# Turning the gated layer's state by block transposes and a trip through DRAM instead of TensorE

## The chip, the cores and the metric

The kernel runs on one core of a Trainium2 chip. A core has TensorE (PE; its weight loads are shown apart as PEld), VectorE (DVE), ScalarE (ACT), GpSimd (POOL) and SyncE (SP, which here only issues transfers). They run at the same time, each takes its own instructions in order, and they wait for each other by semaphores. The metric is the device time of one execution in microseconds.

## The reference

There are 64 graphs of 256 nodes with 128 features, and one dense adjacency matrix of 256 x 256 with numbers in fp32. Four layers follow each other, and each is added to its normed input's source:

```python
h = maximum(layernorm(x), 0)                       # before every layer
# layer 0: five steps of a gated layer
m  = adj @ h                                       # the same for both inputs of the concatenation
z  = sigmoid([m, m] @ w3.T + b3 + h @ u3.T + bu3)
r  = sigmoid([m, m] @ w4.T + b4 + h @ u3.T + bu3)
hv = tanh([m, m] @ w5.T + b5 + (r * h) @ u5.T + bu5)
h  = (1 - z) * h + z * hv
# layer 1: Chebyshev hops of adj up to order 2, then @ Theta1, relu
# layer 2: (adj @ h + h) @ weight + bias, divided by the row's norm
# layer 3: pairwise attention
pre  = s1[i, :] + s2[j, :] + b_lin                 # 256 x 256 x 256 numbers for each graph
e    = leaky_relu(pre, 0.2) @ a + adj
out  = sigmoid(softmax(e) @ h)
```

Layer 3 forms 256 numbers for every pair of nodes of every graph. It is by far the largest part.

## The kernel before, in words

The 64 graphs go in 32 pairs (`NB = 2`). A tensor is held in one of two layouts. By token (`tok`), the partitions are nodes, and the free dimensions are graph of the pair, half of the nodes and feature. By feature (`feat`), the partitions are the 128 features, and the free dimensions are graph and node: 512 numbers in each partition, one PSUM bank.

**The tiles.** Layer 3 is worked in tiles of 128 x 2048 numbers, 128 for each pair and 4096 in all. A tile takes four nodes i, both graphs, all nodes j and one half k of the 256 hidden numbers. It is made by one of three engines: by VectorE in one instruction (line 652, `min` of two operands, the first half k = 0 only), by ScalarE in eight (line 665, either half; from `s2c` for the first half, from a PSUM copy of `s2n` for the second), or by GpSimd in eight (line 672, second half only). TensorE then multiplies it with a window of the vector a and adds it to the scores (line 709, four groups of 32 columns side by side). There are 13 tile buffers; VectorE may hold 8 of them, ScalarE 3 and GpSimd 2.

**The fronts.** Everything before layer 3 is `front(p)`, a generator that goes through layers 0 to 2 for pair p and then makes layer 3's operands. One step of the gated layer goes like this: `mix_nodes` multiplies the state h, by token, with `adj_t` and gives m by feature (TensorE, line 264); ScalarE copies it to mT (line 341); `project` runs five products of 512 columns (line 264); ScalarE applies three tanh (lines 381, 396, 399); VectorE runs four elementwise operations of 512 numbers a partition: rh (line 385), d (line 404), the product with z (line 408) and the new state hT (line 412). The new state is by feature, and the next `mix_nodes` needs it by token as its stationary operand. `to_token` turns it with four 128 x 128 transposes on TensorE (line 292), and ScalarE copies it from PSUM (line 423). The last of the five steps needs the turn for another reason: its result is added to x by token (line 428).

**The tails.** When all 64 tiles of a block of 128 nodes are scored, `tail` adds adj, takes the softmax (lines 558 to 571), turns the weights (line 292), multiplies and stores the result (line 604). There are two tails for each pair. The store's source `o` has two buffers.

**The order.** A planner inside the kernel writes it by hand when the program is built. It keeps a clock for each engine, with a cost for every step (`PROJECT`, `TURN`, `COPY`, `ELEMENTS` and so on). A front or a tail yields before each step the engine it needs and the time from which it can run. When an engine is free the planner takes a tail's step first, then a front's, then a tile. `chain_ready` holds a front back that is more than two steps ahead of its due place, so that it is spread over 1.7 pairs' time. Up to two fronts are under way beside the tiles. `in_order` then ties each engine's instructions to this order. So the order and the share of tiles of each engine are fixed in the program; only the real durations decide how it runs.

**Transfers.** All x loads (line 146), the load of `adj_n` (line 158) and the stores are issued by SP, in the program's order. `xin` has two buffers; `load_x(p + 1)` is called when front p begins. The weights come by ScalarE's queue at the start.

The functions that the change touches, with the profile's line numbers:

Of the kernel before, what the change touches and what calls it, by code (L numbers as in the profile page):

```python
# [8 lines left out]
F32 = mybir.dt.float32  # L9
# [5 lines left out]
P = 128  # L15
NB = 2
STEPS = 5
# [3 lines left out]
PE, DVE, ACT, POOL = ENGINES = (mybir.EngineType.PE, mybir.EngineType.DVE, mybir.EngineType.Activation, mybir.EngineType.Pool)  # L21
# [4 lines left out]
def kernel(  # L26
# [50 lines left out]
    nc = tc.nc  # L77
    B, N, D = x.shape
    NC = N // P
# [4 lines left out]
    const = ctx.enter_context(tc.tile_pool(name="const", bufs=1))  # L84
    work = ctx.enter_context(tc.tile_pool(name="work", bufs=2))
    relu_pool = ctx.enter_context(tc.tile_pool(name="relu", bufs=3))
    psum = ctx.enter_context(tc.tile_pool(name="psum", bufs=1, space=PSUM))
    banks = [psum.tile([P, NB * N], F32, name=f"bank{k}") for k in range(8)]
    s2v = banks[:2]
    s2p = banks[2].rearrange("p (b n) -> p b n", b=NB)  # L90
# [1 line left out]


    clock = dict.fromkeys((PE, DVE, ACT, POOL), 0.0)
    SEEN = {PE: 0.25, DVE: 0.14, ACT: 0.18, POOL: 0.13}
    behind = [0.0]

    def ran(engine, us, *after):
        start = max(clock[engine], 0.0, *after)
        if engine == ACT:  # L100
            behind[0] = max(0.0, behind[0] - (start - clock[ACT])) + 0.024 * us
        clock[engine] = start + us
        return clock[engine] + SEEN[engine] + (behind[0] if engine == ACT else 0.0)

    spare = [[b, 0.0] for b in banks[5:]]

# [5 lines left out]
    def by_feature(b):  # L112
        return b.rearrange("p (b n) -> p b n", b=NB)

    def by_token(b):
        return b.rearrange("p (b c n) -> p b c n", b=NB, c=NC)

    def bank(shape, name):

        spare.append(spare.pop(0))  # L120
        return spare[-1][0][:, :shape[1]]
# [19 lines left out]
    def load_x(p):  # L141
        if p >= NPAIR:
            return
        XIN[p] = work.tile([P, NB, NC, D], F32, name="xin", bufs=2)
        for b in range(NB):
            nc.sync.dma_start(XIN[p][:, b], x[p * NB + b].rearrange("(c p) d -> p c d", p=P))

    load_x(0)


    ident = const.tile([P, P], F32, name="ident")
# [7 lines left out]
    adj_t = const.tile([P, NC, N], F32, name="adj_t")  # L159
    adj_ti = const.tile([P, NC, N], F32, name="adj_ti")  # L160
    for c in range(NC):
        pt = bank([P, N], "pt")
        for k in range(NC):
            nc.tensor.transpose(pt[:, k * P:(k + 1) * P], adj_n[:, k, c * P:(c + 1) * P], ident)
        nc.vector.tensor_copy(adj_t[:, c, :], pt)
        nc.vector.tensor_copy(adj_ti[:, c, :], adj_t[:, c, :])
        nc.vector.tensor_add(adj_ti[:, c, c * P:(c + 1) * P], adj_t[:, c, c * P:(c + 1) * P], ident)


    adj_2 = const.tile([P, NC, N], F32, name="adj_2")  # L170
    for c in range(NC):
        pt = bank([P, N], "pt")
# [76 lines left out]
    pt = bank([P, P], "pt")  # L249
# [16 lines left out]
    def flat(t):  # L266
        return t.rearrange("p b n -> p (b n)")
# [5 lines left out]
    def mix_nodes(pm, h, a):  # L273

        pm = by_feature(pm)
        for b in range(NB):
            for c in range(NC):
                side_by_side(pm[:, b, :], h[:, b, c, :], a[:, c, :], c == 0, c == NC - 1)

    def to_feature(pt, h):  # L280

        pt = by_token(pt)
        for b in range(NB):
            for c in range(NC):
                nc.tensor.transpose(pt[:, b, c, :], h[:, b, c, :], ident)  # L285
# [25 lines left out]
    SHORT = dict(tag="short", bufs=12)  # L311
# [3 lines left out]
    COPY, BIASED, TANH, ELEMENTS = 0.48, 0.58, 0.57, 0.61  # L315
# [34 lines left out]
    def front(p):  # L350
# [7 lines left out]
        h = tok("h", **SHORT)  # L358
        t = yield from norm(x0, 0.0, h)
        yield PE, t, 1  # L360
        b = take()
        to_feature(b[0], h)
        t_h = t
        t = ran(PE, TURN, t, b[1])
        yield ACT, t
        hT, t_hT = copied("hT", b, t)
        for step in range(STEPS):
            yield PE, t_h, 1
            b = take()
            mix_nodes(b[0], h, adj_t)  # L370
            t = ran(PE, MIX, t_h, b[1])
            yield ACT, t
            mT, t_m = copied("mT", b, t)
            yield PE, t_m, 1
            pr = take()
            project(pr[0], u3t, hT, stop=False)
            project(pr[0], w4t, mT, start=False)
            t = ran(PE, 2 * PROJECT, t_m, t_hT, pr[1])
            yield ACT, t, 1
            r = take()  # L380
            nc.scalar.activation(r[0], pr[0], AF.Tanh, bias=br, scale=0.5)  # L381
            t = ran(ACT, TANH, t, r[1])
            yield DVE, t
            rh = feat("rh", **SHORT)
            nc.vector.scalar_tensor_tensor(rh, by_feature(r[0]), 1.0, hT, op0=OP.add, op1=OP.mult)  # L385
            t_rh = ran(DVE, ELEMENTS, t)
            spare.append([r[0], t_rh])
            yield PE, t_rh, 1
            project(pr[0], w34, mT, start=False)
            t_z = ran(PE, PROJECT, t)  # L390
            pv = take()
            project(pv[0], w5t, mT, stop=False)
            project(pv[0], u5t, rh, start=False)
            t = ran(PE, 2 * PROJECT, t_rh, pv[1])
            yield ACT, t_z
            nc.scalar.activation(pr[0], pr[0], AF.Tanh, bias=bz, scale=0.5)  # L396
            t_z = ran(ACT, TANH, t_z)
            yield ACT, t
            nc.scalar.activation(pv[0], pv[0], AF.Tanh, bias=bh, scale=1.0)  # L399
            t = ran(ACT, TANH, t)  # L400

            yield DVE, t
            d = feat("d", **SHORT)
            nc.vector.tensor_sub(d, by_feature(pv[0]), hT)  # L404
            t = ran(DVE, ELEMENTS, t)
            spare.append([pv[0], t])
            yield DVE, max(t_z, clock[DVE])
            nc.vector.scalar_tensor_tensor(by_feature(pr[0]), by_feature(pr[0]), 1.0, d, op0=OP.add, op1=OP.mult)  # L408
            ran(DVE, ELEMENTS, t_z)
            yield DVE, clock[DVE]  # L410
            hT_new = feat("hT", bufs=4)
            nc.vector.scalar_tensor_tensor(hT_new, by_feature(pr[0]), 0.5, hT, op0=OP.mult, op1=OP.add)  # L412
            hT = hT_new
            t_hT = ran(DVE, ELEMENTS)
            spare.append([pr[0], t_hT])
            yield PE, t_hT, 1
            b = take()
            to_token(b[0], hT)
            t = ran(PE, TURN, t_hT, b[1])
            if step < STEPS - 1:  # L420
                yield ACT, t
                h = tok("h", **SHORT)
                nc.scalar.copy(h, by_token(b[0]))  # L423
                t_h = ran(ACT, COPY, t)
                spare.append([b[0], t_h])
# [2 lines left out]
        nc.vector.tensor_add(x1, x0, by_token(b[0]))  # L428
        t = ran(DVE, ELEMENTS, t)
        spare.append([b[0], t])  # L430


        h = tok("h", **SHORT)
        t_h = yield from norm(x1, t, h)
        yield PE, t_h, 1
        b = take()
        mix_nodes(b[0], h, adj_n)
        t = ran(PE, MIX, t_h, b[1])
# [3 lines left out]
        b = take()  # L442
        to_feature(b[0], h)
        t = ran(PE, TURN, t_h, b[1])
        yield ACT, t
        hT, t = copied("hT", b, t)
        yield PE, t_h, 1
        b = take()
        mix_nodes(b[0], h, adj_2)
        t = ran(PE, MIX, t_h, b[1])  # L450
        yield ACT, t
        c2T, t = copied("c2T", b, t)
# [3 lines left out]
        t = ran(PE, PRODUCTS, t, po[1])  # L456
        yield DVE, t
        pt = rows_of(by_token(po[0]))
# [5 lines left out]
        t = ran(DVE, ELEMENTS)  # L464
# [3 lines left out]
        h = tok("h", **SHORT)  # L468
        t = yield from norm(x2, t, h)
        yield PE, t, 1  # L470
        b = take()
        mix_nodes(b[0], h, adj_ti)
        t = ran(PE, MIX, t, b[1])
        yield ACT, t
        yT, t = copied("yT", b, t)
# [3 lines left out]
        t = ran(PE, PRODUCT, t, po[1])  # L479
        yield DVE, t  # L480
        pt = rows_of(by_token(po[0]))
        nc.vector.tensor_add(pt, pt, bias2.unsqueeze(1).to_broadcast([P, NB * NC, D]))
        t = ran(DVE, ELEMENTS, t)
# [3 lines left out]
        t = ran(ACT, COPY, t)  # L487
# [3 lines left out]
        t = ran(DVE, ELEMENTS, t)  # L491
        yield POOL, t
        inverse_root(rn, OP.max, NORM_EPS * NORM_EPS)
        t = ran(POOL, 1.25, t)
# [3 lines left out]
        for k in range(NB * NC):  # L498
            nc.vector.scalar_tensor_tensor(rows_of(x3)[:, k], pt[:, k], rn[:, k:k + 1], rows_of(x2)[:, k],
                                           op0=OP.mult, op1=OP.add)  # L500
        t = ran(DVE, 1.04, t)
# [4 lines left out]
        t = yield from norm(x3, t, h3)  # L506
        yield PE, t, 1
        b = take()
        to_feature(b[0], h3)
        t = ran(PE, TURN, t, b[1])  # L510
        yield ACT, t
        hT, t_hT = copied("hT3", b, t)
# [9 lines left out]
        b = take()  # L522
        project(b[0], g2, hT)
        t = ran(PE, PROJECT, t_hT, b[1])
# [3 lines left out]
        b = take()  # L528
        project(b[0], w2n[:, P:2 * P], hT)
        t = ran(PE, PROJECT, t_hT, b[1])  # L530
# [3 lines left out]
        b = take()  # L534
        project(b[0], adj_t[:, 0, P:2 * P], hT)
        t = ran(PE, PROJECT, t_hT, b[1])
# [6 lines left out]
        b = take()  # L543
        project(b[0], adj_t[:, 0, 0:P], hT)
        t = ran(PE, PROJECT, t_hT, b[1])
# [6 lines left out]
                        since=(max(t_n, t_s2a, t_s2c), max(t_b, t_2)))  # L552
# [172 lines left out]

    def begin_front():
        p = begun_fronts[0]
        load_x(p + 1)
        begin(p, front(p))
        begun_fronts[0] += 1  # L730

# [18 lines left out]

    in_order()
    now = dict.fromkeys(clock, 0.0)
    for e in clock:
        clock[e] = 0.0
    while scored[0] < 2 * NSLOT or CHAINS:
# [4 lines left out]
        for key in CHAINS:  # L760
            since = chain_ready(key, e)
# [6 lines left out]
        else:  # L768
            since = tile_ready(e)
# [47 lines left out]
```

## Time and profile before

| | |
|---|---|
| median of three timed runs | 5358.55 us (5358.25 to 5358.73) |
| the profiled execution | 5354.23 us, of it the span 5352.4 us |
| TensorE clock granted, mean | 0.996 |
| PE busy | 5241.4 us |
| DVE busy | 5221.7 us |
| POOL busy | 5160.9 us |
| ACT busy | 5121.4 us |
| moved by transfers | 26.99 MB, 5 GB/s |

The span is the time from the first to the last instruction of the profiled execution. Busy is the time in which an engine has at least one instruction running. Instructions of one engine overlap a little: the end of one is recorded after the next has begun. So a mean duration is longer than the distance from one start to the next, and where an engine is full the distance is what counts.

### The profile page before, as it was taken

The numbers are of one execution on the slowest core, as the hardware profiler recorded it, in microseconds if no ns is written. First come the engines' busy times: TensorE is split into PE (matmuls) and PEld (weight loads), VectorE is DVE, ScalarE is ACT, GpSimd is POOL, SyncE is SP. The second block draws the span as 40 slices with busy tenths as digits, with TensorE's granted clock in tenths as the row PEclk, the third lists the DMA queues.
The fourth block names the chain that finished last, engine by engine and source line by source line (L and its number), as shares of the span: only waits on it lengthen the run. The fifth ranks groups of instructions, "written<-read, shape, count | busy, mean of one in ns | idle before, by whom it ended". The sixth has DMA issues, their size and how long they took to land.

```text
span 5352.4 us, 138977 instructions
## 1 busy us (share of the span) xinstructions
PE 5241.4 (98%) x56085; PEld 1861.5 (35%) x56085; DVE 5221.7 (98%) x4322; ACT 5121.4 (96%) x13465; POOL 5160.9 (96%) x5974
## 2 busy tenths in 40 slices
PE   6999999999999999999999999999999999999998
PEld 2333333333333333333333333333333333333332
DVE  3999999999999999999999999999999999999998
ACT  3999999999999999999999999999999999999999
POOL 0999999999999999999999999999999999999999
PEclk9999999999999999999999999999999999999999
DMA  0000000000000000000000000000000000000000
GB/s 17 5 5 6 6 3 6 6 5 6 5 4 6 5 6 5 3 6 6 5 5 4 4 6 5 6 6 3 6 5 6 6 5 3 6 5 4 4 2 4
DMA packets 38839, 26.99 MB, mean 5 GB/s; under 512 B 3504, under 2 KB 38192, under 8 KB 38192
## 3 DMA queue, kind: packets, MB, share of 16 engines
q1 hardware_dynamic: 35088, 17.05, 1.1%
q8 instruction: 438, 7.18, 0.6%
q14 instruction: 209, 1.71, 0.1%
q10 hardware_dynamic: 3104, 1.05, 0.1%
HBM read 9.70 MB, written 8.39 MB: 3 GB/s over the span
## 4 chain that ended last, share of the span: by engine, by line
PE 49%; DVE 34%; POOL 9%; ACT 5%; issue 4%; DMA 0%; POOLq 0%; SPq 0%; DVEq 0%; ACTq 0%
PE bank L709 32%; DVE rl L652 28%; PE bank L264 15%; POOL rl L672 7%; ACT rl L665 3%; PE bank L292 1%; DVE d L404 1%; DVE stats L324 1%; DVE bank L408 1%; DVE hT L412 1%; DVE rh L385 1%; PE bank L285 1%; POOL sc L562 0%; DVE mv L327 0%; POOL mv L259 0%
## 5 line engine op out<-in xcount | busy, mean ns | idle before, releaser
L672 POOL TENSOR_SCALAR rl<-s2n,s1b 128x256 f32<-128x256 f32 x5328 | 4786.0, 940 | 9.7 <-ACT s1b L539 9.7
L652 DVE TENSOR_TENSOR rl<-s1a,bank 128x2048 f32<-128x2048 f32 x2015 | 4484.6, 2276 | 12.1 <-ACT s1a L548 12.1
L665 ACT ACTIVATE rl<-bank,s1b 128x256 f32<-128x256 f32 x11056 | 4392.2, 839 | 1.3
L709 PE MATMUL bank<-rl,win_n 128*32 128x512 f32 x21448 | 2654.8, 593 | 33.9 <-DVE rl L652 31.9
L709 PE MATMUL bank<-rl,win 128*32 128x512 f32 x11320 | 1487.2, 593 | 0.0
L709 PEld LDWEIGHTS bank<-rl,win_n 128*32 128x32 f32 x21448 | 678.9, 110 | 1496.4 <-issue 1214.0
L709 PEld LDWEIGHTS bank<-rl,win 128*32 128x32 f32 x11320 | 365.9, 110 | 754.4 <-issue 630.2
L264 PE MATMUL bank<-adj_t,h 128*32 128x256 f32 x5120 | 310.0, 381 | 3.8 <-ACT h L423 3.8
L264 PEld LDWEIGHTS bank<-adj_t,h 128*32 128x32 f32 x5120 | 166.6, 110 | 174.3 <-issue 58.6
L335 ACT ACTIVATE h<-x,mv 128x128 f32<-128x128 f32 x384 | 172.1, 634 | 43.3 <-POOL mv L331 42.9
L264 PE MATMUL bank<-hT,u3t 128*32 128x512 f32 x1280 | 169.5, 593 | 0.0
L264 PE MATMUL bank<-mT,w4t 128*32 128x512 f32 x1280 | 169.4, 592 | 0.0
L264 PE MATMUL bank<-mT,w 128*32 128x512 f32 x1280 | 166.8, 593 | 0.5 <-ACT bank L381 0.5
L264 PE MATMUL bank<-mT,w5t 128*32 128x512 f32 x1280 | 166.7, 592 | 0.4 <-DVE rh L385 0.4
L264 PE MATMUL bank<-rh,u5t 128*32 128x512 f32 x1280 | 166.6, 592 | 0.0
L341 ACT COPY mT<-bank 128x512 f32<-128x512 f32 x160 | 133.9, 837 | 33.1 <-PE bank L264 24.6
L396 ACT ACTIVATE bank<-bank,gate_b 128x512 f32<-128x512 f32 x160 | 141.0, 881 | 17.7 <-PE bank L264 17.7
L381 ACT ACTIVATE bank<-bank,gate_b 128x512 f32<-128x512 f32 x160 | 140.0, 875 | 15.6 <-PE bank L264 15.2
L399 ACT ACTIVATE bank<-bank,gate_b 128x512 f32<-128x512 f32 x160 | 136.3, 852 | 12.8 <-PE bank L264 12.8
L423 ACT COPY h<-bank 128x512 f32<-128x512 f32 x128 | 117.3, 916 | 29.6 <-PE bank L292 24.7
L258 POOL TENSOR_SCALAR mv<-mv 128x4 f32<-128x4 f32 x128 | 29.8, 232 | 120.1 <-DVE mv L326 112.5
L404 DVE TENSOR_TENSOR d<-bank,hT 128x512 f32<-128x512 f32 x160 | 108.4, 678 | 37.5 <-ACT bank L399 37.5
(116 smaller groups left out, 3445.0 us busy)
## 6 DMA issues: line engine op xcount, KB each, us to landing
xin<-in_x_dram SPq DMA_DIRECT2D x64, 128.0 KB, 2.3
out_dram<-o SPq DMA_DIRECT2D x64, 128.0 KB, 1.8
w_raw<-in_L_gnn_w_w_dram ACTq DMA_DIRECT2D x3, 128.0 KB, 4.3
th_raw<-in_L_gnn_Theta_dram ACTq DMA_DIRECT2D x1, 320.0 KB, 3.1
adj_n<-in_adj_dram SPq DMA_DIRECT2D x1, 256.0 KB, 4.8
w_raw<-in_L_gnn_u_w_dram ACTq DMA_DIRECT2D x2, 64.0 KB, 3.4
bias<-in_L_gnn_bias_dram ACTq DMA_DIRECT2D x2, 64.0 KB, 3.0
w<-in_L_gnn_weight_dram ACTq DMA_DIRECT2D x1, 64.0 KB, 2.8
```

The costliest lines, as they stand in the source:

```text
L264: nc.tensor.matmul(o[g:g + 32], w[:, g:g + 32], t, start=start, stop=stop, skip_group_check=True)
L335: nc.scalar.activation(h[:, k, :], s[:, k, :], AF.Relu, bias=mv[:, k, 0:1], scale=mv[:, k, 1:2])
L341: nc.scalar.copy(c, by_feature(bank[0]))
L381: nc.scalar.activation(r[0], pr[0], AF.Tanh, bias=br, scale=0.5)
L396: nc.scalar.activation(pr[0], pr[0], AF.Tanh, bias=bz, scale=0.5)
L399: nc.scalar.activation(pv[0], pv[0], AF.Tanh, bias=bh, scale=1.0)
L404: nc.vector.tensor_sub(d, by_feature(pv[0]), hT)
L423: nc.scalar.copy(h, by_token(b[0]))
L652: nc.vector.tensor_tensor(t, rows.to_broadcast(whole), ops["s2a"].unsqueeze(1).to_broadcast(whole), op=OP.min)
L665: nc.scalar.activation(t[:, g, b, :], (s2p if k else ops["s2c"])[:, b, :], AF.Relu, bias=ops["s1"][k][:, b, i:i + 1], scale=-1.0)
L672: nc.gpsimd.tensor_scalar(t[:, part, b, :], ops["s2n"][:, b, :], ops["s1"][1][:, b, i:i + 1], None, op0=OP.min)
L709: nc.tensor.matmul(pe[g * 32:(g + 1) * 32, :], w[:, k, 31 - r:63 - r], flat(t[:, g]), start=first, stop=(left[block] == 0), skip_group_che ...
```

## The change

Two pairs, p = 0 and 1, keep the old way. For all others, the first four steps of the gated layer no longer use `to_token` and ScalarE's copy. The new function `turned` takes hT, transposes it in blocks of 32 x 32 on VectorE (`blocks`, line 314 of the changed kernel), writes the result to a DRAM buffer (`moves`, line 317) and reads it back in another order (`h_turned`, line 320), so that each partition holds one node of each group of 128. Both transfers are issued by SP. The nodes end up in another order within a group: partition 4 i + c holds node 32 c + i. So `mix_turned` (line 303) multiplies with `adj_p`, a copy of `adj_t` whose rows are put in that order by a product with the permutation `places` during the set-up. It issues as many matmuls of the same size as `mix_nodes`.

The planner books the transpose with `ELEMENTS` (0.61) on VectorE and each transfer with `moved`, 0.5 us of a queue and 2.2 more until the data are there. `blocks` has one buffer, so the planner keeps a transpose until the write before it has been done.

The x loads move as well: the first two pairs' are issued at the very start, ahead of `adj_n`, and `load_x(p + 2)` stands where front p has used its x for the last time.

```diff
+    dram = ctx.enter_context(tc.tile_pool(name="dram", bufs=4, space=bass.MemoryType.DRAM))
...
+    def moved(since):
+        queue[0] = max(queue[0], since) + 0.5
+        return queue[0] + 2.2
...
     load_x(0)
+    load_x(1)
...
+    adj_p = const.tile([P, NC, N], F32, name="adj_p")
+    places = const.tile([P, P], F32, name="places")
+    nc.vector.tensor_copy(places.rearrange("p (i c) -> p i c", c=4), ident.rearrange("p (c i) -> p i c", c=4))
+    for c in range(NC):
+        pt = bank([P, N], "pt")
+        nc.tensor.matmul(pt, places, adj_t[:, c, :])
+        nc.vector.tensor_copy(adj_p[:, c, :], pt)
...
+    def mix_turned(pm, h, a):
+        pm = by_feature(pm)
+        for b in range(NB):
+            for c in range(NC):
+                for g in range(4):
+                    nc.tensor.matmul(pm[g * 32:(g + 1) * 32, b, :], h[:, g, b * NC + c, :], a[:, c, :],
+                                     start=(c == 0), stop=(c == NC - 1), skip_group_check=True)
+
+    t_turn = [0.0]
+
+    def turned(ht, since):
+        yield DVE, max(since, t_turn[0])
+        blocks = work.tile([P, 4, NB * NC, 32], F32, name="blocks", bufs=1)
+        nc.vector.transpose(blocks, flat(ht).rearrange("p (m c j) -> p c m j", c=4, j=32))
+        t = ran(DVE, ELEMENTS, since)
+        moves = dram.tile([P, 4 * P], F32, name="moves")
+        nc.sync.dma_start(moves, blocks.rearrange("p c m j -> p (c m j)"))
+        t_turn[0] = moved(t)
+        h = work.tile([P, 4, NB * NC, 32], F32, name="h_turned", **SHORT)
+        nc.sync.dma_start(h.rearrange("p a m j -> p a (m j)"), moves.rearrange("(a i) (c x) -> (i c) a x", a=4, c=4))
+        return h, moved(t_turn[0])
...
-            mix_nodes(b[0], h, adj_t)
+            if step > 0 and p >= 2:
+                mix_turned(b[0], h, adj_p)
+            else:
+                mix_nodes(b[0], h, adj_t)
...
+            if step < STEPS - 1 and p >= 2:
+                h, t_h = yield from turned(hT, t_hT)
+                continue
             yield PE, t_hT, 1
             b = take()
             to_token(b[0], hT)
...
         spare.append([b[0], t])
+        load_x(p + 2)
...
     def begin_front():
         p = begun_fronts[0]
-        load_x(p + 1)
         begin(p, front(p))
```

More of the change, by code (lines that the diff above doesn't have):

```diff
@@ L94 @@
     clock = dict.fromkeys((PE, DVE, ACT, POOL), 0.0)
+    queue = [0.0]
     SEEN = {PE: 0.25, DVE: 0.14, ACT: 0.18, POOL: 0.13}
@@ L752 @@
     now = dict.fromkeys(clock, 0.0)
+    queue[0] = 0.0
     for e in clock:
```

## The prediction

> **What bounds the kernel now.** I read the page's busy table first, then the busy time by stretch, then the timelines of VectorE and TensorE in mid-run, then the waits.
>
> ```profile
> PE 5241.4 (98%) x56085; PEld 1861.5 (35%) x56085; DVE 5221.7 (98%) x4322; ACT 5121.4 (96%) x13465; POOL 5160.9 (96%) x5974
> ...
> L672 POOL TENSOR_SCALAR rl<-s2n,s1b 128x256 f32<-128x256 f32 x5328 | 4786.0, 940 | 9.7 <-ACT s1b L539 9.7
> L652 DVE TENSOR_TENSOR rl<-s1a,bank 128x2048 f32<-128x2048 f32 x2015 | 4484.6, 2276 | 12.1 <-ACT s1a L548 12.1
> ```
>
> All four engines look full, so the average does not name the bound. By stretch:
>
> ```profile
> 0.00:134.00 134.00, 93.77 (x1021) 39.28 (x1025) 45.00 (x128) 44.09 (x77) 9.28 (x23) 0.90 0.06 17
> ...
> 3000.00:4000.00 1000.00, 992.81 (x10696) 352.73 (x10692) 996.98 (x814) 971.01 (x2561) 990.62 (x1146) 1.00 0.02 5
> ```
>
> The columns are the stretch, then busy us of PE, weight loads, DVE, ACT, POOL. VectorE (DVE) is busy 45.0 of the first 134 us, where two pairs run their gated layers alone: 89 us of idle time. After that it hardly rests. Adding the seven stretches from 268 to 5220 us gives idle times of 18.9 us for DVE, 44.9 for PE, 47.4 for POOL and 124.6 for ACT. Is DVE's busy time real work?
>
> ```profile
> 3049.80 8.87 DVE L652 TENSOR_TENSOR rl<-s1a,bank 128x2048 f32<-128x2048 f32 x4
> 3058.59 0.68 DVE L404 TENSOR_TENSOR d<-bank,hT 128x512 f32<-128x512 f32 x1
> 3059.31 0.70 DVE L408 SCALAR_TENSOR_TENSOR bank<-bank,d 128x512 f32<-128x512 f32 x1
> 3059.92 2.27 DVE L652 TENSOR_TENSOR rl<-s1a,bank 128x2048 f32<-128x2048 f32 x1
> 3062.11 0.68 DVE L412 SCALAR_TENSOR_TENSOR hT<-bank,hT 128x512 f32<-128x512 f32 x1
> ```
>
> Read start to start, as ends overlap the next start. Four tiles take 8.79 us, 2.197 each. A 512-element operation takes 0.60 (L408 to L652: 0.61) when its successor does not need it, but 0.72 (L404 to L408) when the next one reads its result: 0.12 more. No hidden stall is in this. TensorE:
>
> ```profile
> 3016.53 1.04 PE L264 MATMUL bank<-mT,w 128*32 128x512 f32 x8
> 3017.39 1.04 PE L264 MATMUL bank<-mT,w5t 128*32 128x512 f32 x8
> 3018.25 1.04 PE L264 MATMUL bank<-rh,u5t 128*32 128x512 f32 x8
> 3019.22 0.66 PE L292 MATMUL bank<-ident,sc 128*128 128x128 f32 x4
> 3019.81 1.06 PE L709 MATMUL bank<-rl,win 128*32 128x512 f32 x8
> ```
>
> Groups follow every 0.858 us. A turn by transposes takes from 3018.25 + 0.86 = 3019.11 to 3019.81, 0.70 us. PE is nearly gapless too, but the list of waits shows who feeds whom:
>
> ```profile
> PEld bank L709 <- DVE rl L652: 152.2, 271, 4.0
> PEld bank L709 <- ACT rl L665: 96.8, 327, 0.6
> ```
>
> PE waits for tiles, mostly DVE's; DVE waits for nobody. **DVE's fixed stream of instructions sets the pace**, with PE close behind.
>
> [...] No transpose by VectorE is in this trace. [...] L327 works on 4 elements, yet lasts 169 ns at least, 334 at the median and 1697 at most, beside POOL operations of 0.9 us. [...] the transposes (128x128) start 0.11 us after the 32-column groups could have ended, and that is inside the 0.70.
>
> **The change, part by part.** It applies to 30 of 32 pairs, 4 steps each: 120 turns.
>
> *TensorE:* 120 turns of 0.70 go, -84 us. mix_turned issues the same sixteen matmuls as mix_nodes. This shortens the run only as far as PE set the pace; its idle time grows from 44.9 towards 130, and with a longer run beyond.
>
> *ScalarE:* 120 copies (L423) go at 0.47 each (the copy of mT starts at 3006.35, its successor at 3006.82), -56. But the tile shares are frozen when the program is built, and counting its issue order gives DVE 2015 to 1984 tiles, ACT 1415 to 1446, POOL 666 in both. The 31 tiles cost ACT 31 x 8 x 0.476 (busy mean of the form rl<-s2c, 125.7 over 264), +118. Net +62, covered by the 124.6 idle; were that cover gone, tiles would come late to PE, which has slack now.
>
> *VectorE:*
> - 31 tiles fewer at 2.197: -68.1.
> - 120 block transposes of 512 elements. [...] an estimate of 0.63: +75.6. [...]
> - Adjacency. After a turn that takes longer, the chain lags the planner's pacing and its next steps are placed at once. Counting neighbours: L404 directly before L408 66 times before, 125 after; L408 before L412 59 and 119; L459 before L463 7 and 30. That is 142 more pairs at 0.12: +17.0.
> - Set-up: three more copies (0.29 for 128 elements, 0.42 twice for adj_p): +1.1.
>
> Together +25.6.
>
> *The start:* on SP's queue adj_n now stands behind two more loads (two issues took 0.97), so its first transposes come about 1 us later: +1. The two matmuls for adj_p (0.67 each by the row of L174) run while DVE is still waiting for PE.
>
> *Transfers.* A turn writes 256 KB and reads them back. The loads of 128 KB land after 2.3 us, the stores after 1.8. [...] The planner books 0.5 + 2.2 twice, 5.4. I cost this at nothing: PE has work placed between, and a pause of PE is taken from its new slack of about 4 us a pair. Without that cover it is rival C. [...] a store is needed only two tails later (o has two buffers, a tail comes every 82 us). The x loads move to where their buffer comes free. Before, SP sat up to 89 us in front of one (L146 <- DVE x L428), and now it can't hold the moves up. The single blocks buffer makes a transpose wait for the write before it; turns come 41 us apart on average (four in each 164 us of a pair), so it costs nothing unless two fronts collide.
>
> **The sum.** Profiled execution 5354.2 (span 5352.4 and 1.8 around it) + 25.6 + 1 = 5380.8. The median of the timed runs is 4.3 above it, so 5385 us, 0.5% slower. About 0.2% (10.7 us) is what a measurement of this kernel can tell from no change.
>
> **Rivals.**
> A, the forecast, 0.55: DVE stays the pace, 5385, by itself 5370 to 5405.
> B, no visible change, 0.18: the transpose costs 0.60 (72) and the adjacency finds its room in the 18.9 us of idle time: -68 + 72 + 2 gives 5365. For it: those gaps are part of the same idle time. Against: a gap of 0.035 accounts for only a third of the 0.12.
> C, a new wait, 0.12: the data come 1 us later than booked. PE stands in order at mix_turned, the copy of mT and the gates follow late, and DVE stands at rh (L385). Half a microsecond at each of 120 turns: +60, 5445. For it: the chain's steps are now placed with no spare time. [...]
> D, a dear transpose, 0.10: [...]
> E, faster, 0.05: PE is the real pace and DVE follows. Then 84 us of PE work are worth up to 84, until DVE's own work binds: [...] It decides if DVE's added work stays below the idle time that a freer PE gives back. Against: DVE waits for PE almost nowhere. Faster is also open only through DVE's work, as POOL's is unchanged to the tile.
> That the change isn't made is excluded: the built program holds 120 transposes and 240 transfers.
>
> Chances: faster 0.06 (E and the edge of B), same 0.19 (B), slower 0.75 (A, C, D). The range runs from B's lower edge, 5350, to C and D, 5450.
>
> **What would show it.** Right: DVE 99% or more busy in mid-run with about 25 us more in all, the transpose's row at 0.7 us mean and 0.63 start to start, PE's idle time near 150 us (44.9 + 84 + 26), POOL as before. C shows as PE waiting for h_turned and DVE's L385 rows waiting for ACT; D in the transpose's mean. Wrong: DVE's idle time falling by more than its work rises, or DVE idle while PE is full.

## The result, and the profile after

The changed kernel takes 5385.38 us in the median of five timed runs (5381.66 to 5386.52), against 5358.55 us of the kernel before on the same chip (five runs, 5358.25 to 5359.57). The ratio is 1.0048, with a 95% interval from 1.0037 to 1.0059: the change costs 26.8 us. The span of the profiled execution grew from 5352.4 to 5383.6 us.

The page of the changed kernel: first the busy table, then the rows of the tiles on GpSimd and VectorE (busy us, mean ns, then the idle time ahead of them).

```profile
PE 5197.7 (97%) x55609; PEld 1833.3 (34%) x55609; DVE 5236.3 (97%) x4414; ACT 5156.6 (96%) x13593; POOL 5167.3 (96%) x5974
...
L722 POOL TENSOR_SCALAR rl<-s2n,s1b 128x256 f32<-128x256 f32 x5328 | 4791.0, 923 | 14.6 <-ACT s1b L589 9.5
...
L702 DVE TENSOR_TENSOR rl<-s1a,bank 128x2048 f32<-128x2048 f32 x1984 | 4410.7, 2273 | 12.4 <-ACT s1a L598 12.0
```

TensorE lost 43.7 us of busy time and no time was won by it. GpSimd makes the same 5328 operations. VectorE makes 31 tiles fewer and is still busy for 14.6 us more (5221.7 to 5236.3), because of this row, from the list of its groups:

```profile
L314 DVE STREAM_TRANSPOSE blocks<-hT 128x512 f32<-128x512 f32 x120 | 84.4, 704 | 0.0
```

The busy time by stretch (PE, weight loads, DVE, ACT, POOL) of the changed kernel, and below it mid-run in one stretch, first of the kernel before, then of the changed kernel:

```profile
0.00:134.00 134.00, 92.14 (x1018) 39.67 (x1018) 46.05 (x131) 42.46 (x74) 9.30 (x23) 0.91 0.06 17
...
3000.00:4000.00 1000.00, 976.94 (x10512) 341.59 (x10508) 989.22 (x833) 973.40 (x2570) 984.88 (x1138) 0.99 0.06 17
```

```profile
268.00:5220.00 4952.00, 4907.14 (x52726) 1745.65 (x52720) 4933.11 (x4027) 4827.38 (x12721) 4904.62 (x5669) 1.00 0.02 5
```

```profile
268.00:5220.00 4952.00, 4838.67 (x52067) 1706.85 (x52063) 4917.36 (x4098) 4837.51 (x12784) 4884.99 (x5640) 1.00 0.05 17
```

TensorE now has 113 us without work from 268 to 5220 us, where it had 44.9; that is as much as ScalarE has (114.5). VectorE is still nearly full, yet its idle time in the same window rose from 18.9 to 34.7 us, and GpSimd's from 47.4 to 67.0. The clock granted to TensorE was 0.993 in the mean, against 0.996; its products of 512 columns have the same recorded means (592 to 593 ns in the page before, 592 to 594 now), so slower matmuls are not seen.

VectorE's waits in this window, of the kernel before (one line is above 0.4 us) and of the changed kernel, say whom it waited for, us in all, times and the longest:

```profile
DVE nmx L566 <- POOL sc L562: 8.9, 17, 1.0
```

```profile
DVE sc L608 <- PE bank L759: 10.8, 12, 2.0
DVE rh L431 <- ACT bank L427: 4.7, 5, 1.3
DVE nmx L616 <- POOL sc L612: 2.0, 4, 0.8
```

In all these lists come to 10.0 us before and 21.5 us after. So the growth between the two profiled executions, 31.2 us, is 14.6 us of work on VectorE and 16.6 us in which it stands: of these some 4 are short gaps ahead of dependent operations, and 11.5 are new waits in mid-run (by the lists, which leave out gaps under 0.15 us).

The timeline of VectorE in mid-run shows the new operation and its neighbours:

```profile
3013.16 0.68 DVE L450 TENSOR_TENSOR d<-bank,hT 128x512 f32<-128x512 f32 x1
3013.88 0.70 DVE L454 SCALAR_TENSOR_TENSOR bank<-bank,d 128x512 f32<-128x512 f32 x1
3014.61 0.69 DVE L458 SCALAR_TENSOR_TENSOR hT<-bank,hT 128x512 f32<-128x512 f32 x1
3015.22 2.28 DVE L702 TENSOR_TENSOR rl<-s1a,bank 128x2048 f32<-128x2048 f32 x1
3017.41 0.70 DVE L314 STREAM_TRANSPOSE blocks<-hT 128x512 f32<-128x512 f32 x1
3018.04 13.24 DVE L702 TENSOR_TENSOR rl<-s1a,bank 128x2048 f32<-128x2048 f32 x6
```

From the transpose's start to its successor's are 0.63 us. The dependent operations L450, L454 and L458 now stand side by side, with 0.72 and 0.73 us from start to start. The list of waits:

```profile
PEld bank L759 <- DVE rl L702: 272.9, 356, 4.0
PEld bank L759 <- ACT rl L715: 152.0, 510, 0.7
...
PEld bank L303 <- DMA h_turned<-moves: 76.0, 67, 4.0
...
PE bank L303 <- DMA h_turned<-moves: 33.9, 28, 3.1
```

TensorE waits longer for VectorE's tiles than before (272.9 against 152.2 us), and for the turned state 110 us in all. The transfers' own list gives the time from issue to landing in its last column:

```profile
moves<-blocks SPq DMA_DIRECT2D x120, 256.0 KB, 2.0
h_turned<-moves SPq DMA_DIRECT2D x120, 256.0 KB, 2.8
```

The turn at 3017.41 us goes the whole way in about the time that the planner books. It has its write issued at 3018.15 and its read at 3020.22; TensorE begins with it at 3023.49, after 6.1 us. The planner books 0.61 + 0.14 + 5.4 = 6.15. Over all 120 turns this way takes 5.5 to 10.6 us, with a median of 6.4, which includes the time in which TensorE is not yet free for it.

### The profile page after: what moved, and what is told of

It is laid out like the page before. It is cut to its first block, busy times and chain, and to the rows that moved or that the text cites. A ratio compares the mean times of both kernels' runs of the same rounds, so it can differ in the third digit from the quotient of the medians.

```text
span 5383.6 us, 138419 instructions
## 1 busy us (share of the span) xinstructions
PE 5197.7 (97%) x55609; PEld 1833.3 (34%) x55609; DVE 5236.3 (97%) x4414; ACT 5156.6 (96%) x13593; POOL 5167.3 (96%) x5974
## 4 chain that ended last, share of the span: by engine, by line
PE 34%; DVE 30%; POOL 8%; ACT 8%; issue 5%; DMA 1%; SPq 0%; POOLq 0%; DVEq 0%; ACTq 0%
DVE rl L702 24%; PE bank L759 22%; PE bank L281 9%; POOL rl L722 7%; ACT rl L715 6%; PE bank L303 2%; DMA h_turned<-moves 1%; DVE stats L367 1%; DVE bank L454 1%; DVE d L450 1%; DVE rh L431 1%; DVE blocks L314 0%; DMA moves<-blocks 0%; DVE hT L458 0%; PE bank L328 0%
## 5 line engine op out<-in xcount | busy, mean ns | idle before, releaser
L722 POOL TENSOR_SCALAR rl<-s2n,s1b 128x256 f32<-128x256 f32 x5328 | 4791.0, 923 | 14.6 <-ACT s1b L589 9.5
L702 DVE TENSOR_TENSOR rl<-s1a,bank 128x2048 f32<-128x2048 f32 x1984 | 4410.7, 2273 | 12.4 <-ACT s1a L598 12.0
L759 PE MATMUL bank<-rl,win 128*32 128x512 f32 x11568 | 1540.1, 594 | 0.0
L759 PEld LDWEIGHTS bank<-rl,win 128*32 128x32 f32 x11568 | 383.1, 110 | 801.8 <-issue 615.5
L303 PE MATMUL bank<-adj_p,h_turned 128*32 128x256 f32 x3840 | 240.0, 390 | 34.2 <-DMA h_turned<-moves 33.9
L715 ACT ACTIVATE rl<-s2c,s1a 128x256 f32<-128x256 f32 x512 | 239.8, 912 | 0.0
L442 ACT ACTIVATE bank<-bank,gate_b 128x512 f32<-128x512 f32 x160 | 157.4, 984 | 39.9 <-PE bank L281 39.5
L427 ACT ACTIVATE bank<-bank,gate_b 128x512 f32<-128x512 f32 x160 | 167.3, 1045 | 22.6 <-PE bank L281 21.5
L445 ACT ACTIVATE bank<-bank,gate_b 128x512 f32<-128x512 f32 x160 | 149.7, 935 | 35.5 <-PE bank L281 35.4
L303 PEld LDWEIGHTS bank<-adj_p,h_turned 128*32 128x32 f32 x3840 | 123.2, 112 | 169.8 <-DMA h_turned<-moves 76.0
L384 ACT COPY mT<-bank 128x512 f32<-128x512 f32 x160 | 150.2, 939 | 31.4 <-PE bank L303 15.0
L450 DVE TENSOR_TENSOR d<-bank,hT 128x512 f32<-128x512 f32 x160 | 108.9, 680 | 39.3 <-ACT bank L445 39.3
```

What stands on the lines that cost most here:

```text
L303: nc.tensor.matmul(pm[g * 32:(g + 1) * 32, b, :], h[:, g, b * NC + c, :], a[:, c, :], start=(c == 0), stop=(c == NC - 1), skip_group_check ...
L384: nc.scalar.copy(c, by_feature(bank[0]))
L702: nc.vector.tensor_tensor(t, rows.to_broadcast(whole), ops["s2a"].unsqueeze(1).to_broadcast(whole), op=OP.min)
L715: nc.scalar.activation(t[:, g, b, :], (s2p if k else ops["s2c"])[:, b, :], AF.Relu, bias=ops["s1"][k][:, b, i:i + 1], scale=-1.0)
L722: nc.gpsimd.tensor_scalar(t[:, part, b, :], ops["s2n"][:, b, :], ops["s1"][1][:, b, i:i + 1], None, op0=OP.min)
L759: nc.tensor.matmul(pe[g * 32:(g + 1) * 32, :], w[:, k, 31 - r:63 - r], flat(t[:, g]), start=first, stop=(left[block] == 0), skip_group_che ...
```

## The experiments

The kernels of one group ran on one chip with the kernel before, whose median was 5347.6 us in the first two groups and 5359.0 us in the third. So kernels of different groups are compared by their ratios to it.

### First group: take one cost away, or double it

**Without the block transposes** (`no_transpose`):

```diff
-        blocks = work.tile([P, 4, NB * NC, 32], F32, name="blocks", bufs=1)
-        nc.vector.transpose(blocks, flat(ht).rearrange("p (m c j) -> p c m j", c=4, j=32))
...
-        nc.sync.dma_start(moves, blocks.rearrange("p c m j -> p (c m j)"))
+        nc.sync.dma_start(moves, flat(ht))
```

> The changed kernel without its 120 block transposes: the state is written to DRAM as it is, so the blocks reach the next product unturned (this part of the computation is left out). The order of all other instructions is the same. If VectorE's stream sets the pace, 120 x 0.63 = 76 us of its work go, and what comes next is GpSimd, with about 65 us idle in mid-run: 5385 - 76 to - 60, so 5309 to 5325. If the waits for the transfers set it, only the earlier start of the transfers counts: 5340 to 5370. If TensorE sets it, no change, 5385.

Measured: ratio 1.0021 (1.0012 to 1.0029), 5359 us. Against the changed kernel (1.0052 on this chip, below; 1.0048 as first measured) that is 14 to 17 us less, not 60 to 76, and not nothing either. It lies in the range of the second expectation, 5340 to 5370, near its upper edge when it is brought to the first chip by the ratios (5369). The transfers' part can't be set aside: TensorE's waits for the turned state fell with the transposes, from 107 us in the repeated run of the changed kernel to 16. VectorE's waits from 268 to 5220 us show why the rest did not come back (in this run's kernel the lines are numbered two lower, so L606 is L608 above):

```profile
DVE sc L606 <- PE bank L757: 12.9, 20, 1.6
DVE nmx L614 <- POOL sc L610: 10.6, 16, 1.3
DVE x L547 <- POOL rn L276: 9.5, 12, 1.6
DVE rh L429 <- ACT bank L425: 6.8, 11, 2.1
```

(Engine and line, whom it waits for: us in all, times, longest.) VectorE now stands 60 us in this window and waits for the others, most of all for GpSimd: 20.1 us. Another bound lies close below VectorE's. How much of the 14 to 17 us is the transposes' work and how much the earlier data, this run does not tell.

**With every transpose done twice** (`two_transposes`):

```diff
         nc.vector.transpose(blocks, flat(ht).rearrange("p (m c j) -> p c m j", c=4, j=32))
+        nc.vector.transpose(blocks, flat(ht).rearrange("p (m c j) -> p c m j", c=4, j=32))
```

> The changed kernel with every block transpose done twice in a row into the same buffer; all other instructions in the same order. If VectorE's stream sets the pace: 5385 + 120 x 0.63 (0.70 if the second has to wait for the first) = 5461 to 5470. If TensorE sets it, 5385 to 5400, since its idle time would take up the rest.

Measured: 1.0194 (1.018 to 1.0208), 5452.15 us. That is 0.0142 to 0.0146 above the changed kernel, 76 to 78 us for 120 more transposes, 0.63 to 0.65 us each. Added to the changed kernel, VectorE's work went into the time one to one.

**Without the transfers** (`no_transfers`):

```diff
-        moves = dram.tile([P, 4 * P], F32, name="moves")
-        nc.sync.dma_start(moves, blocks.rearrange("p c m j -> p (c m j)"))
...
-        h = work.tile([P, 4, NB * NC, 32], F32, name="h_turned", **SHORT)
-        nc.sync.dma_start(h.rearrange(...), moves.rearrange(...))
+        h = adj_n.rearrange("p c n -> p (c n)").rearrange("p (a m j) -> p a m j", a=4, j=32)
```

> The changed kernel with the transposes but without the 240 transfers: the next product takes a constant tile as its state (the steps' result does not reach the next step by this way). Same order. It takes away TensorE's 110 us of recorded waits for the state and SP's issues. If VectorE's stream sets the pace, only the part of these waits that reaches VectorE comes back, about 10 us: 5370 to 5380. If the waits for transfers are what the change costs: 5330 to 5355.

Measured: 1.0026 (1.0017 to 1.0036), 5361.41 us: 12 to 15 us less than the changed kernel. All of TensorE's waits for the turned state are gone, and about an eighth of them comes back. This is an upper bound of what the transfers cost, since the product no longer waits for hT and the transpose either. The trace says where it came from: against the repeated run of the changed kernel VectorE's busy time is the same (5230.6 and 5230.7 us), and its idle time in the whole span is 9.4 us less (137.0 to 127.6). Its listed waits in mid-run fell from 11.1 to 2.8 us; the largest of the repeated run, which have gone, were these:

```profile
DVE sc L608 <- PE bank L759: 6.2, 10, 1.5
DVE rh L431 <- ACT bank L427: 2.6, 3, 1.0
```

**The kernel before with the changed start** (`before_start`):

```diff
     load_x(0)
+    load_x(1)
...
+    adj_p = const.tile([P, NC, N], F32, name="adj_p")
+    ...                                  # places and the two products, as in the change
...
-        load_x(p + 1)
+        if p:
+            load_x(p + 1)
```

> The kernel before with the changed kernel's start alone: the second pair's x loaded ahead of the adjacency, and the permuted copy of it computed (and not used). Same order elsewhere. The trace of the changed kernel shows the first norm at 22.7 us against 19.3 us: 3.4 us more, 5362. If the start were covered by later idle time: 5358.5.

Measured: 1.0005 (0.9997 to 1.0013), 2.7 us. In the trace the first norm starts at 22.94 us, 3.7 us later than before. The time agrees with that, but its interval holds zero as well, so the timing leaves it open.

### Second group: neighbours and late data

**The changed kernel again** (`after_again`), for comparison on this chip:

> The changed kernel itself, so that the following kernels are compared with it on one chip: 1.0048 times the kernel before, as first measured.

Measured: 1.0052 (1.0039 to 1.0065), 5376.82 us.

**Dependent operations kept apart** (`after_spaced`, and the same in the kernel before, `before_spaced`):

```diff
-            yield DVE, max(t_z, clock[DVE])
+            yield DVE, max(t_z, clock[DVE] + SEEN[DVE])
...
-            ran(DVE, ELEMENTS, t_z)
-            yield DVE, clock[DVE]
+            t = ran(DVE, ELEMENTS, t_z)
+            yield DVE, t
```

and likewise before x2.

> The changed kernel, in which the planner may place the second and third of VectorE's dependent operations (the product with z, the new state, and the residual after the first bias) only 0.14 us after the one before them, so that a tile mostly comes between: dependent neighbours of 512 elements fall from 282 to 36. Tile shares 1982, 1448 and 666 instead of 1984, 1446 and 666. If VectorE's work sets the pace and a dependent neighbour costs 0.12 us: up to 246 x 0.12 = 30 us less, but the run without transposes gained only 14 us before other engines took over, so 10 to 20 us less, ratio to before 1.001 to 1.003. If the adjacency costs nothing because its gaps lie in idle time, or if a later chain brings new waits: no gain or slower, 1.005 or more.

> The same spacing in the kernel before: dependent neighbours of 512 elements fall from 140 to 28, tile shares 2014, 1419 and 663 instead of 2015, 1415 and 666. If VectorE's work sets the pace: 112 x 0.12 = 13 us and one tile, 2 us, less, ratio 0.997. If TensorE sets the pace of the kernel before, no change, 1.000.

Measured: 1.0048 (1.0036 to 1.0061) for the changed kernel, which is no gain that can be told, and 0.9979 (0.9971 to 0.9988), 11 us less, for the kernel before. In the changed kernel VectorE's busy time fell by 15 us (5230.6 to 5215.6), but its idle time from 268 to 5220 us rose from 24 to 40. So what VectorE saved came back as idle time. The new orders move tiles too: two from VectorE in the changed kernel (4.4 us of the 15), and in the kernel before one from VectorE and three, 22 us, from GpSimd. So neither run shows the spacing alone.

**The transfers booked later** (`late_booking`):

```diff
-        return queue[0] + 2.2
+        return queue[0] + 3.0
```

> The changed kernel with the planner's booking of each transfer raised by 0.8 us (3.0 instead of 2.2 until the data are there, 7.0 instead of 5.4 for a turn), so that the next product is placed later in TensorE's order. Tile shares 1985, 1444 and 667; dependent neighbours 310 instead of 282. If the late data cost about 12 us, as the run without transfers says, most of that comes back and the neighbours take 3: 5 to 9 us less, ratio to before 1.003 to 1.004. If that run gained by the missing transfers and not by the waits, no change: 1.005.

Measured: 1.0053 (1.0039 to 1.0066), no change. TensorE's waits for the turned state did fall, from 107 us in the repeated run of the changed kernel to 27:

```profile
PE bank L303 <- DMA h_turned<-moves: 8.8, 6, 4.6
...
PEld bank L303 <- DMA h_turned<-moves: 18.1, 12, 5.5
```

That nothing came back does not show that the waits cost nothing, because the new order also gave a tile more to GpSimd (busy 5153.6 to 5160.8 us) and one more to VectorE, with 28 more dependent neighbours (5230.6 to 5236.9 us). A gain of some us can be hidden behind these. Whether the run without transfers gained by the waits or by something else that went with them, such as the freedom from hT, stays open.

### Third group: GpSimd, and other shares

**Less work for GpSimd**, in the kernel without transposes (`no_transpose_pool`) and in the changed kernel (`after_pool`):

```diff
-        nc.gpsimd.tensor_scalar(o, o, 0.5, 0.5, op0=OP.mult, op1=OP.add)
```

> The kernel without the block transposes, and without GpSimd's scaling of the output by 0.5 plus 0.5 (line 651, 64 operations of 0.41 us, some 24 us; left out as well). In the run without transposes GpSimd's idle time from 268 to 5220 us was 54 us, of which about 42 lie in gaps between its dependent small operations that every run has, the kernel before too; so it would be within 12 us of its own limit. If GpSimd is the next bound below VectorE, its 24 us come back for the most part: from 1.0021 to 0.998 to 1.000. If it is ScalarE, or the waits between the engines' orders as such: no change, 1.002.

> The changed kernel without the same 24 us of GpSimd's work and nothing else changed. If VectorE's stream sets the pace of the changed kernel, GpSimd's work is beside it: 0 to 5 us less, ratio to before 1.004 to 1.005. If GpSimd sets it too: 15 to 24 us less, 1.001 to 1.002.

Measured: 0.9943 (0.9929 to 0.9957) and 1.0012 (1.0003 to 1.002). Without the transposes, leaving the operation out brings 42 us (1.0021 to 0.9943; the two intervals together allow 33 to 51). The 64 operations take 25.9 us, and there are short gaps around them: in these two runs GpSimd's busy time differs by 14.8 us (5153.1 and 5138.3), since its other operations are recorded as longer, and its short gaps in mid-run by another 14.7. So 42 us came back for some 29 us of GpSimd's time. VectorE's busy time fell by 11 us as well (5183.8 to 5172.4); whether this makes the rest is not shown. That GpSimd's work counts in full once the transposes are gone is shown; that it is the only bound there is not. And the second expectation failed: in the changed kernel itself, too, leaving it out brings 19 to 21 us. VectorE does not set the pace alone. Counted from the changed kernel at 1.0052, the transposes alone are worth 17 us, GpSimd's operation alone 21, and both together 58. That is 20 us more than the parts, and the four intervals together allow 8 to 32. Two full engines that wait for each other by turns would behave so: relieving one soon stops at the other. That reading is argued from the waits.

How they do it is seen in GpSimd's waits from 268 to 5220 us, first of the kernel before, then of the changed kernel (the repeated run):

```profile
POOL sc L562 <- DVE sc L558: 2.3, 4, 0.8
POOL rn L258 <- DVE rn L490: 2.2, 1, 2.2
POOL mv L258 <- DVE mv L326: 0.9, 2, 0.5
POOL o L601 <- ACT o L597: 0.4, 1, 0.4
```

```profile
POOL mv L275 <- DVE mv L369: 12.7, 15, 2.3
POOL sc L612 <- DVE sc L608: 4.3, 7, 1.6
```

Before, GpSimd waited 5.8 us in this window for anybody. The rest of its 47.4 us idle, 41.6 us, are short gaps, most of them around its small dependent operations. The same remainder is 41.6 us in the repeated run of the changed kernel, 41.5 without the transposes and 41.6 in the spaced kernel before, whatever the other engines did there (38.5 with every transpose done twice). So GpSimd was as full as VectorE. In the changed kernel it waits for VectorE's statistics and scores.

**Other shares** (`after_shifted`, `before_shifted`): the spacing, and two costs of the planner set a little higher, so that ScalarE takes more tiles. In the changed kernel the start was mended as well.

```diff
-            done = ran(DVE, 2.2, since)
+            done = ran(DVE, 2.23, since)
...
-            done = ran(POOL, 1.8, since)
+            done = ran(POOL, 1.83, since)
```

> The changed kernel with its start mended (x of the second pair loaded behind the adjacency, the permuted copy made at the end of the set-up), the spacing, and the planner told that a tile takes VectorE 2.23 instead of 2.2 us and a part of one GpSimd 1.83 instead of 1.8: tile shares 1967, 1470 and 659 instead of 1984, 1446 and 666, all results as before. Against the changed kernel VectorE has 17 tiles x 2.2 = 37 us and up to 226 x 0.12 = 27 us less, GpSimd 7 x 7.2 = 50 us less, ScalarE 24 x 2.9 = 70 us more of 107 us idle, and TensorE has the slack of the turns that left it. If VectorE and then GpSimd set the pace: 35 to 60 us less than the changed kernel, ratio to before 0.994 to 0.998. If the turns' latency or ScalarE holds it up: 1.002 or more.

> The kernel before with the spacing and the same two numbers told to the planner: tile shares 2001, 1437 and 658 instead of 2015, 1415 and 666, results as before. VectorE has 14 x 2.2 + 112 x 0.12 = 44 us less, GpSimd 58 us less, ScalarE 22 x 2.9 = 64 us more of 125 us idle; TensorE keeps its turns and has 45 us idle from 268 to 5220 us. If TensorE is the next bound here: 20 to 40 us less, 0.993 to 0.996. If ScalarE binds first: no better than the spaced one, 0.998.

Measured: 1.0072 (1.0059 to 1.0084), slower than the changed kernel, and 0.9932 (0.9919 to 0.9944), 37 us faster than the kernel before, for the spacing, the two costs and the tiles that they moved together. **This last version, with TensorE's turns, is the fastest of all that compute the whole result.** Its busy table:

```profile
PE 5255.0 (99%) x56085; PEld 1893.0 (36%) x56085; DVE 5174.6 (97%) x4308; ACT 5177.3 (97%) x13641; POOL 5110.0 (96%) x5910
```

The shifted version of the changed kernel failed where I expected the gain. From 268 to 5220 us, VectorE and GpSimd stand and wait for ScalarE in it, and ScalarE waits for the product of the turned state (the lines are numbered one higher here):

```profile
DVE rh L432 <- ACT bank L428: 30.3, 15, 13.1
DVE d L451 <- ACT bank L446: 20.2, 12, 6.6
```

```profile
POOL rl L723 <- ACT s1b L590: 28.2, 6, 8.9
```

```profile
ACT mT L385 <- PE bank L304: 19.8, 11, 6.5
```

ScalarE is busy 4890.6 of these 4952 us. In the version with TensorE's turns it is busier still, 4913.95, and nobody waits as long. So it isn't ScalarE's load alone. The single waits of 6 us and more, behind the product of the turned state, speak for the long way of the turn, which a full ScalarE can't make up for. That is argued from the trace and was not tried apart.

## Why the prediction was right

The forecast was 5385 us; 5385.38 were measured. The direction holds, and so does the main link: VectorE has more to do, though it makes fewer tiles. That the sum fits to less than 1 us is in part luck. VectorE's added work, with its short gaps, was forecast at 25.6 us; the traces show 14.6 us of busy time and some 4 to 5 of short gaps, 19 in all. New waits of VectorE, forecast at nothing, make 11.5 us. And the profiled execution was forecast at 5380.8 us and came at 5385.4, while the 4.3 us that were added for the timed runs did not appear, since this execution was itself the median.

| step | predicted | shown |
|---|---|---|
| 31 tiles fewer | -68.1 | three tiles in 6.59 us (3031.81 to 3038.40), 2.197 each, as taken |
| 120 transposes at 0.63 | +75.6 | 0.63 start to start; doubling them costs 76 to 78, leaving them out brings 14 to 17 |
| 142 dependent neighbours | +17.0 | 0.12 each in the trace; taking most of them away brings nothing that can be told in the changed kernel |
| set-up and start | +2.1 | the first norm 3.4 us later; timed alone +2.7, zero not excluded |
| transfers, and waits of VectorE | 0 | 12 to 15 without transfers; VectorE's waits in mid-run 10.0 to 21.5 |
| sum | +26.6 | +26.8 timed, +31.2 between the profiled executions |

Of ScalarE's +62 us, which the forecast left out of the sum as covered, 35 are seen in its busy time (5121.4 to 5156.6), and its idle time in mid-run fell by only 10 us, so it was covered. The start was dearer than forecast because the two products for `adj_p` were not hidden: VectorE's next operation behind them (L192, L175 before) began at 14.02 us instead of 10.15, while its first copy of the adjacency, ahead of them, came at 7.82 instead of 7.35.

**The transposes** were the unknown: there was none by VectorE to read from, and the forecast's 0.63 us for one was its author's estimate. The nearest that the trace before shows is 0.61 us, from the start of L408, which also has 512 numbers a partition, to that of the tile behind it. Measured: 0.63 us from start to start, in fp32. Rival D, a dear transpose, is out: doubling them costs 0.63 to 0.65 us each, and all 120 last between 690 and 706 ns. GpSimd is busy 4885.0 of the 4952 us from 268 to 5220 in the changed kernel's trace, and a transpose held up beside it is not seen. L370, with 4 elements, lasts from 169 to 1764 ns in it, 259 at the median; what makes some of these long was not shown.

**The transfers.** That the two of a turn keep to the 5.4 us which the planner books was the author's estimate: the trace before has loads and stores of 128 KB (2.3 and 1.8 us at the median) and a single load of 256 KB, at the start (4.8 us). Measured are 2.0 us at the median for the write of 256 KB and 2.8 for the read, 4.8 together. Rival C, data later than booked, happened in part: TensorE waited 110 us for them. But the next link, that VectorE stands at rh, came to 4.7 us in mid-run (L431 waiting for L427) instead of 60. TensorE's new slack took up most of it, as the forecast's main case said, but not all: VectorE's waits for TensorE and ScalarE rose with it, as shown above.

**Where the reading was off.** "DVE's fixed stream of instructions sets the pace", with PE close behind, is half of it. The engine beside VectorE is GpSimd. Its 47.4 us of idle time in mid-run were not looked into; 41.6 of them are gaps that remained in the other runs too. The question that I asked of VectorE, whether its busy time is real work, should have been asked of GpSimd's idle time. The forecast did not suffer, because the change adds work to VectorE and leaves GpSimd's alone, and work added to VectorE went into the time in full (76 to 78 us with every transpose doubled). My first expectation after it, that taking the transposes away would return 60 to 76 us, did suffer: it returned 14 to 17.

**The adjacency term** is the other soft one. Its 0.12 us is plain in the trace, and the gaps ahead of these two operations (L454 and L458, L408 and L412 before) rose from 4.3 to 8.4 us in the list of groups. Whether it makes 17 us of the changed kernel's time isn't shown: with 36 neighbours instead of 282 VectorE worked 15 us less and stood 16 us more. What the run without transfers returned is of the same size. This stays open.

**Rivals B and E.** No visible change is excluded by the interval, which begins at 1.0037. E, that TensorE is the real pace, is excluded for the changed kernel by the run with doubled transposes: TensorE already had 113 us of pauses, and 76 us more of VectorE's work still went into the time in full. The predicted idle time of TensorE near 150 us was too high. Its busy time fell by 43.7 us and not by 84, probably because a group's recorded end (1.04 us) reaches 0.18 us over the distance to the next one (0.858), so that shorter pauses are not seen as idle time.

## What to carry to other kernels

Where several engines are full, ask of each engine's idle time what it consists of: gaps that stay whatever the others do are no room, and GpSimd with 1% idle time was here as much the bound as VectorE with 0.4%. Work put on a full engine went into the time in full here (76 to 78 us for 120 more transposes of 0.63), though TensorE's saving was larger; work taken off a full engine came back only in part (14 to 17 us of 76), since the next one was close. A sum that fits is not yet an account: look for the new waits of the pacing engine, even where they were forecast at nothing. When the order is planned ahead, try first what the planner's own costs do to the shares: two numbers changed by under 2% and a spacing of 0.14 us together brought 37 us here, more than the whole change cost.

## What the runs showed that I had not expected

- A block transpose of 128 x 512 in fp32 takes 0.63 us from start to start, 690 to 706 ns recorded in all 120, with GpSimd busy 4885.0 of 4952 us in mid-run.
- Writing 256 KB from the chip's SBUF to DRAM lands in 2.0 us at the median, reading them back in 512-byte pieces in 2.8. SP needs 0.33 and 0.36 us to issue them.
- Relief of two full engines came to more than its parts: 17 and 21 us alone, 58 us together, with an interval of 8 to 32 us for the difference.
- The kernel before differs by 0.2% between the chips of the second and the third group: medians of 5347.6 and 5359.0 us.
